# Media keys and values of all rows inside the integer attention, media statistics row by row, two buffers of routed rows

## The chip, the cores and the metric

The kernel runs on one core of a Trainium2 chip. The metric is the device time of one execution in microseconds (us), the median of three runs: 3255.36 us, from 3247.82 to 3256.58. The engines are named as in the profile: PE (TensorE, matmuls), PEld (its weight loads), DVE (VectorE), ACT (ScalarE), POOL (GpSimd) and SP (SyncE, which here only issues DMAs).

## What is computed

A decoder layer stack on `x` of 8 batch rows x 512 tokens x 256 channels, all in fp32. Every step adds to `x` what it computes from a layer norm of `x`:

```python
x = x + self_attention(LN(x))
x = x + cross_attention(LN(x), ctx_1024, adj, mask)
x = x + local_transformer(LN(x))              # depth 2, with feed-forward
x = x + integer_attention(LN(x))              # 16 heads, over the batch axis
x = x + media_attention(LN(x), ctx_1024, key_mask)
x = x + mixture_of_experts(LN(x))             # top 1 of 8, capacity 512, FF 1024
```

The change lies in the fourth and the fifth step, and in the routing that opens the sixth. The two that matter, cut:

```python
# integer attention (T = 8 rows, B = 512 tokens, E = 256)
xq, xs = quant_act(query, 8)                  # scale by the maximum over all of it, round
q, k, v = quant_linear(xq, ...) ; each quantized by its own maximum
aw = quant_act(einsum('ntd,nsd->nts', q, k)) ; probs = quant_act(int_softmax(aw))
attn = quant_act(einsum('nts,nsd->ntd', probs, v)) ; out = quant_linear(attn, wo)

# media attention (8 heads of 64; its own layer norm on top of the outer one)
xn = (x - mu) * rsqrt(var + eps) * gamma + beta
q = xn @ Wq * scale ; k, v = split(media @ Wkv)       # media = ctx_1024
out = softmax(mask(q k^T)) v @ Wout
```

Keys and values of the media attention depend on `ctx_1024` and `Wkv` alone, and not on `x`: they can be computed at any time once those are loaded. Each maximum in the integer attention is one over the whole tensor, so each of its sub-stages ends before the next begins.

## The kernel before

One core works through the stages one after the other in `fast_stages` (L3201). Of interest are `stage_quantized_attention` (L2257), `stage_media_attention` (L2664), `routing` (L2867) and `stage_moe` (L3018). `x` stays on the chip as 32 tiles of 128 tokens, four to a batch row. Engines have their own in-order instruction streams; a program schedules the order within each stream at build time, and semaphores join them. Tiles come from pools with a set number of buffers: a new tile of a name waits until the one that used its buffer is done with.

**The integer attention** is split by its pools:

- qa1/qp1: `rows` (L2298) makes integer rows of the normalised `x` (POOL and DVE L2307, DVE L2311, ACT L2312), transposes them on PE (L2315) and copies them by ACT (L2319). `channels` (L2284) multiplies them by the integer weights in PSUM tiles `pj` (3 buffers); `largest` (L2324) takes their maxima on DVE (L2326). Then queries, keys and values.
- qa2/qp2: scores, with their maxima in `aw`, a tile of four quarters' room that is first written here.
- qa3/qp3: `integer_softmax`, and in the same pools `keys_values` (L2586), which has nothing to do with it: it makes the *media* keys and values of batch rows 1 to 5 (`AHEAD`). Five contexts are loaded by SP into `qa_big`, a tile not yet in use. Then come 40 groups of two program matmuls on PE (L2608), each one evacuated by an ACT copy (L2610) into `kv_o` and stored in `kv`, a tensor in DRAM (L2611). One program matmul in fp32 of this kind appears in the trace as two records.
- qa4/qp4, the weighing phase: a loop of nine steps. `spread` (L2475) spreads values by POOL and DVE copies (L2478); `turn` (L2483) scales scores (DVE L2485), makes four shifted versions (ACT L2488), transposes them on PE (L2496) into PSUM tiles `tr` (4 buffers) and copies them back by DVE (L2499); `weigh` (L2501), one step behind, multiplies by the values (PE L2509), copies by ACT (L2517) and takes a maximum on DVE (L2518).
- qa5/qp5: rounding, transposes, and for each batch row b the output projection, its scaling by DVE into `qa_o` (L2575) and the addition to `x` (L2577), on DVE for odd b and on POOL for even b.

**The media attention** first takes the statistics of all 32 tiles (`ln_stats`: DVE L141, L142, then the inverse root in small operations, L1458 to L1462) and from them those of its second layer norm (L2684 to L2688). `prepare(b)` is a list of pieces of work for row b: `load` (the DMAs and the normalisation into `ma_xn`, L155), for rows 0, 6 and 7 the keys (four groups, L2726) and values (four groups, L2734), then two transposes (`turn`, L2713, and DVE L2719) and four groups of queries (L2726). For rows 1 to 5 the load reads `kv` from DRAM instead (L2701).

The loop runs 16 steps for each row. A step has the scores of a pair of heads for 128 keys (PE L2758), their exponent (ACT L2763) and the running sum: for the first of four steps a copy on POOL (L2769), else an addition on DVE (L2771). Two steps later PE weighs the values (L2781). In each step but the first, one piece of `prepare` for the next row is done. All of row 0's pieces run ahead of the loop, and the output projection and its addition to `x` (L2838, L2843) follow behind.

**The routing** of a row follows its output projection in pieces that fall due at set steps of the loop: statistics, the normalised rows into `mo_rows` (DVE L155; a copy of `x` and a count by POOL, L2906 and L2907), transposes, router logits (L2925), the choice of an expert, the place in it, and four indirect DMAs issued by POOL (L2988) that send the rows from `mo_rows` to `slots` in DRAM. `mo_rows` has one buffer. `stage_moe` reads `slots` when all sends are done.

Of the kernel before, what the change touches and what calls it, by code (L numbers as in the profile page):

```python
# [26 lines left out]
F32 = mybir.dt.float32  # L27
# [10 lines left out]
P = 128  # L38
# [1237 lines left out]
class FastDecoder(Decoder):  # L1276
# [980 lines left out]
    def stage_quantized_attention(self, w):  # L2257
# [3 lines left out]
        with tc.tile_pool(reuse_waits="tile", name="qa", bufs=1) as pool:  # L2261
# [17 lines left out]
            with tc.tile_pool(reuse_waits="tile", name="qa1", bufs=2) as tmp, tc.tile_pool(  # L2279
                reuse_waits="tile", name="qp1", bufs=1, space=PSUM  # L2280
            ) as psum:
                part = self.alloc(tmp, [P, B, 6], F32, "qa_part", bufs=1)

# [168 lines left out]
            with tc.tile_pool(reuse_waits="tile", name="qa3", bufs=2) as tmp, tc.tile_pool(  # L2452
                reuse_waits="tile", name="qp3", bufs=4, space=PSUM
            ) as psum:
                ptop = self.integer_softmax(tmp, aw, qs, atop)
                room = self.alloc(pool, [P, 8, 2, S], F32, "qa_big")
                self.keys_values(tmp, psum, room)

                ps_, _ = self.scaled(pool, ptop, 1.0 / 128.0 / 127.0, "qa_ps")
                pr = one("qa_pr")  # L2460
                nc.vector.reciprocal(pr, ptop)
                nc.vector.tensor_scalar(pr, pr, 127.0, None, ALU.mult)
# [7 lines left out]
            with tc.tile_pool(reuse_waits="tile", name="qa4", bufs=2) as tmp, tc.tile_pool(  # L2470
# [50 lines left out]

                for n in range(9):
                    if n < 8:
                        spread(n)
                        turn(n)
                    if n:
                        weigh(n - 1)

# [14 lines left out]
            with tc.tile_pool(reuse_waits="tile", name="qa5", bufs=2) as tmp, tc.tile_pool(  # L2543
# [22 lines left out]
                for b in range(B):  # L2566
# [10 lines left out]
                    (nc.vector if b % 2 else nc.gpsimd).tensor_tensor(x, x, o, ALU.add)  # L2577
# [6 lines left out]
    AHEAD = range(1, 6)  # L2584

    def keys_values(self, pool, psum, room):  # L2586
# [3 lines left out]
        self.kv = self.alloc(self.dram, [B, 2, P, NST * S], F32, "kv")  # L2590
        for n, b in enumerate(self.AHEAD):
            ctxT = room[:, n]
            nc.sync.dma_start(
                ctxT, t["ctxT"].rearrange("(k p) n -> p k n", p=P)[:, :, b * S : (b + 1) * S]
            )
        for n, b in enumerate(self.AHEAD):
            ctxT = room[:, n]
            for j in range(2):
                for g in range(NST):
                    ps = self.alloc(psum, [P, S], F32, "kv")  # L2600
                    for k in range(2):
                        at = slice(g * P, (g + 1) * P)
                        w, x = wkv[:, k, j * S : (j + 1) * S], ctxT[:, k, :]
                        if j == 0:
                            w = w[:, at]
                        else:
                            w, x = x[:, at], w
                        nc.tensor.matmul(ps, w, x, start=(k == 0), stop=(k == 1))  # L2608
                    o = self.alloc(pool, [P, S], F32, "kv_o", bufs=3)
                    nc.scalar.copy(o, ps)  # L2610
                    nc.sync.dma_start(self.kv[b, j][:, g * S : (g + 1) * S], o)  # L2611
# [52 lines left out]
    def stage_media_attention(self, w, out):  # L2664
# [5 lines left out]
        with self.tc.tile_pool(reuse_waits="tile", name="ma", bufs=2) as pool, self.tc.tile_pool(  # L2670
# [8 lines left out]


            mean, rstd, var = self.ln_stats(pool, lambda i: [self.x[:, i, :]], NT, "ma_ln", with_var=True)
            var2 = self.alloc(pool, [P, NT], F32, "ma_var2", bufs=1)
            rstd2 = self.alloc(pool, [P, NT], F32, "ma_rstd2", bufs=1)
            nc.vector.tensor_tensor(var2, var, rstd, ALU.mult)  # L2684
            nc.vector.tensor_tensor(var2, var2, rstd, ALU.mult)
            nc.vector.tensor_scalar(var2, var2, EPS, None, ALU.add)
            self.rsqrt(pool, rstd2, var2, "ma_t2")
            nc.vector.tensor_tensor(rstd2, rstd2, rstd, ALU.mult)  # L2688
            stats = mean, rstd2
# [3 lines left out]
            def prepare(b):  # L2693
                d = held[b] = {}

                def load():
                    d["k"] = self.alloc(pool, [P, 4, S], F32, "ma_kT")
                    d["v"] = self.alloc(pool, [P, NST, S], F32, "ma_v")
                    if b in self.AHEAD:
                        for j, n in enumerate("kv"):  # L2700
                            nc.sync.dma_start(d[n].rearrange("p a n -> p (a n)"), self.kv[b, j])  # L2701
                    else:
                        d["ctxT"] = self.alloc(pool, [P, 2, S], F32, "ma_ctxT")
                        nc.sync.dma_start(
                            d["ctxT"], t["ctxT"].rearrange("(k p) n -> p k n", p=P)[:, :, b * S : (b + 1) * S]
                        )
                    d["xn"] = self.alloc(pool, [P, NST, C], F32, "ma_xn", bufs=1)
                    for i in range(NST):
                        self.normalize(d["xn"][:, i, :], self.x[:, b * NST + i, :], stats, b * NST + i)
# [21 lines left out]
                def values(i):  # L2731
                    ps = self.alloc(psum, [P, 512], F32, "pj", bufs=2)
                    for k in range(2):
                        nc.tensor.matmul(  # L2734
                            ps, d["ctxT"][:, k, i * P : (i + 1) * P], wkv[:, k, S:],
                            start=(k == 0), stop=(k == 1),
                        )
                    self.evac(d["v"][:, i, :], ps)

                yield load  # L2740
                if b not in self.AHEAD:
                    for g in range(4):
                        yield lambda g=g: project(d["k"], wkv, d["ctxT"], g)
                    for i in range(NST):
                        yield lambda i=i: values(i)
# [120 lines left out]

    def routing(self, pool, psum, later, out):  # L2867
# [18 lines left out]
        def route(b):  # L2886
# [15 lines left out]
            def norm():  # L2902
                rows = d["rows"] = self.alloc(pool, [P, NST, self.WIDE], F32, "mo_rows", bufs=1)
# [466 lines left out]
```

## Time and profile before

| what | us |
| --- | --- |
| runs | 3247.82, 3256.58, 3255.36 |
| the profiled execution | 3254.52 |
| its span | 3252.6 |
| the 40 key and value groups of rows 1 to 5 (first to last ACT copy) | 2331.7 to 2399.8 |
| the weighing phase, qa4 | 2403.9 to 2442.4 |
| the last addition to `x` in the integer attention ends | 2481.1 |
| first scores of the media loop | 2511.64 |
| its rows open (POOL L2769) | 2515.33, 2555.63, 2608.16, 2663.18, 2718.19, 2774.16, 2843.62, 2913.08 |
| row 7's sends are issued | 3000.16 to 3005.0 |

Times count from the start of the span. In the page of the whole execution the engines are busy as follows (time, share of the span, number of instructions):

```profile
PE 2954.8 (91%) x15008; PEld 1502.6 (46%) x15008; DVE 2126.2 (65%) x4594; ACT 1148.2 (35%) x1599; POOL 415.7 (13%) x384
```

PE's share is a mean over all stages, of which some keep it full and some do not. Matmuls are pipelined and their ends are modelled, so what one takes out of the stream is read from the distance of two starts rather than from its length. An entry of the timeline or of the groups names the line, the engine, the operation, and what is written from what.

### The profile page before, as it was taken

Reading aid. Unit: us, or ns where it says so; the run is one execution under the profiler, and the core shown is the slowest. Engines: PE = TensorE matmul, PEld = TensorE weight load, DVE = VectorE, ACT = ScalarE, POOL = GpSimd, SP = SyncE. Lnnn points to the kernel's source line nnn. Section 1 sums busy time; section 2 is a strip of 40 time slices with the busy share of each in tenths; the row PEclk is TensorE's granted clock in tenths of the full one; section 3 lists DMA queues with packets and bytes.
Section 4 is the critical chain, followed back from the end, with each engine's and each line's share of the span. In section 5 each row is a group of like instructions: output and inputs, shape, how many; then the busy total and the mean of one; then the engine's idle time right before and its main releaser. Section 6 shows DMA issues by size and latency. Waiting matters only on the chain. (4 is left out here: it accounts for less than half of the span.)

```text
span 3252.6 us, 39809 instructions
## 1 busy us (share of the span) xinstructions
PE 2954.8 (91%) x15008; PEld 1502.6 (46%) x15008; DVE 2126.2 (65%) x4594; ACT 1148.2 (35%) x1599; POOL 415.7 (13%) x384
## 2 busy tenths in 40 slices
PE   8998888878998999999999999997876999996998
PEld 5642232224554555555454555554443333333665
DVE  6458888877878854466887858648798465555110
ACT  2146566643344321124334321113362443332111
POOL 1111001010011010000110111102211222222111
PEclk9999999989999999999999999998888999998999
DMA  7011111101000010001000011000321122112431
GB/s 230 1 58 44 57 52 39 39 16 53 15 21 21 17 46 14 1 1 37 17 21 15 21 41 59 20 7 26 105 86 46 53 99 79 34 35 78 121 135 58
DMA packets 122176, 155.82 MB, mean 48 GB/s; under 512 B 46742, under 2 KB 74477, under 8 KB 120694
## 3 DMA queue, kind: packets, MB, share of 16 engines
q1 hardware_dynamic: 117878, 141.59, 14.0%
q0 software_dynamic: 4096, 11.59, 1.0%
q8 instruction: 120, 1.97, 0.2%
q14 instruction: 82, 0.67, 0.1%
HBM read 106.66 MB, written 41.21 MB: 45 GB/s over the span
## 5 line engine op out<-in xcount | busy, mean ns | idle before, releaser
L1810 PE MATMUL pj<-w,la_hT 128*128 128x512 f32 x720 | 347.7, 615 | 23.4 <-DVE la_v L1815 21.2
L1662 DVE TENSOR_TENSOR x_e<-x_e,x_share 128x1024 f32<-128x1024 f32 x256 | 306.8, 1243 | 25.5 <-ACT x_e L1661 24.8
L1661 ACT ACTIVATE x_e<-sc 128x1024 f32<-128x1024 f32 x256 | 249.7, 1025 | 148.7 <-PE sc L1650 146.2
L2763 ACT ACTIVATE ma_e<-sc,ma_bias 128x1024 f32<-128x1024 f32 x128 | 142.4, 1114 | 200.9 <-PE sc L2758 192.6
L2771 DVE TENSOR_TENSOR ma_esum<-ma_esum,ma_e 128x1024 f32<-128x1024 f32 x96 | 122.4, 1275 | 134.9 <-ACT ma_e L2763 129.1
L1810 PEld LDWEIGHTS pj<-w,la_hT 128*128 128x128 f32 x720 | 129.8, 191 | 167.5 <-issue 119.3
L3113 POOL TENSOR_TENSOR la_oT<-la_o,x_wide 128x512 f32<-128x512 f32 x64 | 97.5, 1535 | 795.5 <-DMA x_wide<-invs 591.9
L1931 ACT ACTIVATE la_e<-la_e 128x1024 f32<-128x1024 f32 (+1 forms) x128 | 121.5, 951 | 182.5 <-DVE la_e L1927 182.5
L2095 ACT ACTIVATE lf_gate<-pj,lf_b 128x512 f32<-128x512 f32 (+1 forms) x82 | 56.3, 687 | 359.4 <-PE pj L2074 359.4
L1677 PE MATMUL po<-x_e,x_v 128*32 128x512 f32 x1024 | 143.5, 634 | 33.4 <-DVE x_e L1662 31.4
L2074 PE MATMUL pj<-lf_hnT,w 128*128 128x512 f32 (+1 forms) x368 | 173.5, 598 | 0.0
L1927 DVE TENSOR_TENSOR la_e<-sc,la_mask 128x1024 f32<-128x1024 f32 (+1 forms) x128 | 138.4, 1082 | 44.7 <-PE sc L1920 44.6
L1650 PE MATMUL sc<-x_q,x_k 32*128 32x512 f32 x1024 | 159.5, 663 | 0.3 <-ACT x_e L1661 0.2
L2074 PE MATMUL sc<-lf_hnT,w 128*128 128x512 f32 x336 | 155.9, 592 | 0.0
L2142 PE MATMUL po<-w,lf_hid 128*128 128x256 f32 x640 | 153.9, 386 | 0.0
L2758 PE MATMUL sc<-ma_qT,ma_kT 64*128 64x512 f32 x512 | 144.2, 641 | 0.7 <-ACT ma_e L2763 0.7
L1986 PE MATMUL pj<-w,la_oT 128*128 128x256 f32 x512 | 124.3, 389 | 22.0 <-ACT la_qkT L1856 12.6
L2781 PE MATMUL po<-ma_e,ma_v 128*64 128x512 f32 x512 | 138.1, 618 | 0.0
L1920 PE MATMUL sc<-la_qkT 64*128 64x256 f32 (+1 forms) x1024 | 134.2, 380 | 1.2 <-DVE la_e L1927 1.2
L2142 PEld LDWEIGHTS po<-w,lf_hid 128*128 128x128 f32 x640 | 117.3, 190 | 34.6 <-issue 20.4
L1938 PE MATMUL po<-la_e,la_v 128*64 128x256 f32 (+1 forms) x1024 | 129.0, 373 | 3.8 <-ACT la_o L1960 3.8
L1817 ACT ACTIVATE la_sq<-pj 128x512 f32<-128x512 f32 x120 | 71.4, 595 | 156.2 <-PE pj L1810 156.1
(486 smaller groups left out, 5206.3 us busy)
## 6 DMA issues: line engine op xcount, KB each, us to landing
x_wide<-invs SPq DMA_DIRECT2D x184, 128.0 KB
w<-in_f_w_dram SPq DMA_DIRECT2D x16, 1024.0 KB
kv<-kv_o SPq DMA_DIRECT2D x40, 256.0 KB
slots<-x_empty SPq DMA_DIRECT2D x8, 1028.0 KB
x_mask<-in_x_maskT_dram SPq DMA_DIRECT2D x8, 1024.0 KB
ex_rows<-slots SPq DMA_DIRECT2D x7, 1028.0 KB
ma_kT<-kv SPq DMA_DIRECT2D x5, 1024.0 KB
ma_v<-kv SPq DMA_DIRECT2D x5, 1024.0 KB
```

The costliest lines, as they stand in the source:

```text
L1650: nc.tensor.matmul(pair[r // 2][:, r % 2, :], d["k"][rows, g, kt * P : (kt + 1) * P], d["q"][rows, e, g, :], start=True, stop=True,)
L1661: nc.scalar.activation(ex, d["e"][rest][p], AF.Exp)
L1662: nc.vector.tensor_tensor(ex, ex, d["share"][:, kt, :].unsqueeze(1).broadcast_to([P, 2, 512]), ALU.mult)
L1677: nc.tensor.matmul(d["po"][32 * r : 32 * r + 32, :], d["v"][:, kt, 8 * g + 2 * r + e, :], ex[r // 2][:, r % 2, :], start=(kt == 0), stop=( ...
L1810: nc.tensor.matmul(ps, d["hT"][:, k, i * P : (i + 1) * P], wqkv[:, k, j * S : (j + 1) * S], start=(k == 0), stop=(k == 1),)
L1920: nc.tensor.matmul(ps[:, r, jj * 256 : jj * 256 + to - j * P], d["qkT"][rows, 4 + c, j * P : (j + 1) * P], d["qkT"][rows, c, j * P : to], ...
L1927: nc.vector.tensor_tensor(ex[:, :, :n_cols], ps[:, :, :n_cols], mask[:, :n_cols].unsqueeze(1).broadcast_to([P, 2, n_cols]), ALU.add,)
L2074: nc.tensor.matmul(ps[:m, :], w1[:, k, at : at + m], held[b]["hnT"][:, k, :], start=(k == 0), stop=(k == 1))
L2142: nc.tensor.matmul(ps[:, :C], src[:, i * P : (i + 1) * P], w2[: src.shape[0], f, :], start=(f == 0), stop=last_f,)
L2758: nc.tensor.matmul(ps[:, r, :], d["k"][rows, c, kt * P : (kt + 1) * P], d["q"][rows, c, :], start=True, stop=True,)
L2763: nc.scalar.activation(ex, ps, AF.Exp, bias=bias[:, b * NST + kt : b * NST + kt + 1], scale=0.125)
L2781: nc.tensor.matmul(d["po"][64 * r : 64 * r + 64, :], d["v"][:, kt, 128 * c + 64 * r : 128 * c + 64 * r + 64], ex[:, r, :], start=(kt == 0) ...
```

## The change

1. `keys_values` becomes a generator that takes the rows to do, the room for their contexts, the PSUM tag and the buffers, and that yields after each group. It is called three times:
   - for row 0 at the start of qa1, with PSUM tiles `pj`, two groups in each. The context lies in one quarter of the unused `aw`, and the ACT copies write the other three quarters in turn. That is 32 records on PE, four ACT copies of 128x1024, one context load and four stores on SP.
   - for rows 1 to 5 where it was, at once, as before.
   - for rows 6 and 7 in the nine-step loop of qa4, two groups in each step until the 16 are done, with PSUM tiles of the transposes' tag `tr`, `kv_o` in three buffers, and one buffer for the context.
2. The media loop loads keys and values of all rows from `kv`; its own groups for rows 0, 6 and 7 are gone.
3. The additions to `x` of the integer attention run on POOL for b = 2, 4, 6 and on DVE for the others.
4. The media statistics are taken for one row at a time (`twice_normal`): for row 0 directly after its addition to `x`, for rows 1 to 7 in their `load`.
5. `mo_rows` has two buffers (the pool's own number).

The core of the diff:

```diff
@@ stage_quantized_attention, qa1
+                self.kv = self.alloc(self.dram, [B, 2, P, NST * S], F32, "kv")
+                free = aw.rearrange("p n r a s -> p (n r a s)").rearrange("p (i k n) -> p i k n", i=4, k=2)
+                outs = itertools.cycle([free[:, i] for i in range(1, 4)])
+                for _ in self.keys_values(tmp, psum, range(1), free, "pj", 3, outs):
+                    pass
@@ qa3
-                self.keys_values(tmp, psum, room)
+                for _ in self.keys_values(tmp, psum, range(1, 6), room, "kv", 4):
+                    pass
@@ qa4
+                ahead = self.keys_values(tmp, psum, range(6, B), None, "tr", 4)
                 for n in range(9):
                     if n < 8:
                         spread(n)
                         turn(n)
                     if n:
                         weigh(n - 1)
+                    for _ in range(2):
+                        next(ahead, None)
@@ qa5
-                    (nc.vector if b % 2 else nc.gpsimd).tensor_tensor(x, x, o, ALU.add)
+                    (nc.gpsimd if b in (2, 4, 6) else nc.vector).tensor_tensor(x, x, o, ALU.add)
+                    if b == 0:
+                        self.media_stats = {b: self.twice_normal(tmp, b, self.const)}
@@ keys_values
+        if room is not None:
+            ctxs = [context(room[:, i], b) for i, b in enumerate(rows)]
+        for i, b in enumerate(rows):
+            if room is None:
+                ctxT = context(self.alloc(pool, [P, 2, S], F32, "kv_ctx", bufs=1), b)
+            else:
+                ctxT = ctxs[i]
             for j in range(2):
-                for g in range(NST):
-                    ps = self.alloc(psum, [P, S], F32, "kv")
...
+                for g in range(0, NST, n):
+                    ps = self.alloc(psum, [P, n, S], F32, tag, bufs=bufs)
...
+                    yield
@@ stage_media_attention
-            mean, rstd, var = self.ln_stats(pool, lambda i: [self.x[:, i, :]], NT, "ma_ln", with_var=True)
...
-                    if b in self.AHEAD:
-                        for j, n in enumerate("kv"):
-                            nc.sync.dma_start(d[n].rearrange("p a n -> p (a n)"), self.kv[b, j])
...
+                    for j, n in enumerate("kv"):
+                        nc.sync.dma_start(d[n].rearrange("p a n -> p (a n)"), self.kv[b, j])
+                    stats = self.media_stats.pop(b, None) or self.twice_normal(pool, b)
...
-                if b not in self.AHEAD:
-                    for g in range(4):
-                        yield lambda g=g: project(d["k"], wkv, d["ctxT"], g)
-                    for i in range(NST):
-                        yield lambda i=i: values(i)
@@ twice_normal (new)
+        mean, rstd, var = self.ln_stats(
+            pool, lambda i: [self.x[:, b * NST + i, :]], NST, "ma_ln", with_var=True
+        )
...
+        nc.vector.tensor_tensor(var2, var, rstd, ALU.mult)
+        nc.vector.tensor_tensor(var2, var2, rstd, ALU.mult)
+        nc.vector.tensor_scalar(var2, var2, EPS, None, ALU.add)
+        self.rsqrt(pool, rstd2, var2, "ma_t2")
...
@@ routing, norm
-                rows = d["rows"] = self.alloc(pool, [P, NST, self.WIDE], F32, "mo_rows", bufs=1)
+                rows = d["rows"] = self.alloc(pool, [P, NST, self.WIDE], F32, "mo_rows")
```

## The prediction, made before the changed kernel ran

> **What bounds the kernel now.** I read the busy times by stage first, because the mean (PE 91%) hides two regimes. Columns: window, its length, then for PE, weight load, DVE, ACT and POOL the busy time with its count, granted clock, DMA share, GB/s.
>
> ```profile
> 2200.50:2213.50 13.00, 0.00 (x0) 0.00 (x0) 7.92 (x30) 1.10 (x2) 1.10 (x2) 0.63 0.48 161
> 2213.50:2221.00 7.50, 5.64 (x30) 3.19 (x30) 6.55 (x12) 4.16 (x5) 2.80 (x1) 0.50 0.01 2
> 2403.00:2442.50 39.50, 19.51 (x640) 16.25 (x640) 34.35 (x50) 30.56 (x40) 13.38 (x13) 0.71 0.02 3
> 2481.00:2501.00 20.00, 14.07 (x26) 5.76 (x25) 19.25 (x98) 1.76 (x3) 0.37 (x2) 0.84 0.23 88
> 2516.00:2774.00 258.00, 257.38 (x1038) 92.05 (x1034) 148.49 (x294) 108.49 (x120) 63.00 (x57) 1.00 0.22 73
> 2774.00:2913.00 139.00, 139.00 (x523) 53.10 (x523) 72.67 (x152) 49.18 (x59) 30.35 (x28) 1.00 0.12 39
> ```
>
> The media loop (last two rows) has no idle PE time: a matmul removed there is time removed. At the start of the integer attention PE is idle for 13 us, in its weighing phase (2403 to 2442.5) it works half the time while DVE works 34.35 of 39.5, and in the prologue of media (2481 to 2501) DVE is the full engine. So the change moves PE work from a place where PE sets the end to places where something else does.
>
> Next, the timeline of POOL, whose copies open every head pair; these open rows 3 to 7:
>
> ```profile
> 2663.18 1.04 POOL L2769 COPY ma_esum<-ma_e 128x1024 f32<-128x1024 f32 x1 [8.40 <-ACT ma_e L2763]
> 2718.19 1.04 POOL L2769 COPY ma_esum<-ma_e 128x1024 f32<-128x1024 f32 x1 [8.40 <-ACT ma_e L2763]
> 2774.16 1.04 POOL L2769 COPY ma_esum<-ma_e 128x1024 f32<-128x1024 f32 x1 [8.21 <-ACT ma_e L2763]
> 2843.62 1.04 POOL L2769 COPY ma_esum<-ma_e 128x1024 f32<-128x1024 f32 x1 [15.46 <-ACT ma_e L2763]
> 2913.08 1.04 POOL L2769 COPY ma_esum<-ma_e 128x1024 f32<-128x1024 f32 x1 [15.76 <-ACT ma_e L2763]
> ```
>
> Row 3 takes 55.01 (2718.19 - 2663.18); rows 5 and 6, which prepare rows 6 and 7 with their own keys and values, take 69.46 and 69.46.
>
> Then the chain of waits at the end of the loop:
>
> ```profile
> 2797.20 1.91 PE pj L2734 x4
> 2931.83 4.07 DMA slots<-mo_rows,mo_to
> 2981.59 5.68 DMA slots<-mo_rows,mo_to
> ```
>
> The same places in the timelines (start, duration, what, in brackets the idle time before it and who ended it):
>
> ```profile
> 2936.06 0.15 POOL L2907 IOTA mo_rows<- 128x4 f32 x1 [2.81 <-DMA slots<-mo_rows,mo_to]
> 2987.40 2.18 DVE L155 TENSOR_SCALAR mo_rows<-x,mo_ln_mean,mo_ln_rstd 128x256 f32<-128x256 f32 x4 [9.82 <-DMA slots<-mo_rows,mo_to]
> 2500.92 1.38 DVE L155 TENSOR_SCALAR ma_xn<-x,ma_ln_mean,ma_rstd 128x256 f32<-128x256 f32 x4
> ```
>
> Twice the chain runs through the sends of routed rows, because the next row's `mo_rows` needs their buffer; and row 0's normalisation starts at 2500.92, 20 us after the last x add ended (2481.1).
>
> **Media loop, rows 6 and 7.** Their 16 groups leave a full PE. Measured by rows: 2 x (69.46 - 55.01) = **-28.9**. By the chain, 16 pieces like the first above, 16 x 1.91 = -30.6; I keep -26 (a tenth of it turning up as other waits) as the other end. The 2 x 2 loads of 1 MB replace two of 512 KB; rows 1 to 5 have such loads already and show no wait for them.
>
> **Two buffers of routed rows.** DVE's normalisation of row 7 (L155) stood 9.82 behind row 6's sends, till 2987.40. With a second buffer its inputs are ready at 2977.6: **-9.8** (-5 if the new sends queue behind row 6's on POOL, -10.5 at best). The stall at 2936.06, 2.81 behind row 5's sends, goes too: **-2.8** (0 to -4.1, the chain's piece). Late next: the router's matmuls, then row 7's own sends.
>
> **Prologue.** Before, DVE finishes the x adds at 2481.1, takes the statistics of all 32 tiles until 2493.6 and two inverse roots until 2500.9. After, DVE counts from its first qa_o at 2462.41: two qa_o 2.4; x rows 0 and 1 at 1.2 each, which is the same-shaped add L2771's price with POOL elsewhere, 2.4; four tiles' statistics at 0.39, 1.6; three pairs of (two qa_o 2.34 + an add beside POOL's, 2.35), 14.1; 27 small dependent operations at 0.20 (the pace of the 128x4 chain in the routing), 5.4. Sum 25.9, so xn at 2488.3, 12.6 earlier. PE then does no keys and values (they filled 2479.4 to 2503 and were hidden behind DVE), so it arrives cold: at 2494.4 half clock lasted 3.2 us after an idle gap, half of that lost, 1.6. Together **-11** (-6 if half clock holds through all 16 query records, +6.8, -12.6, say -13, without any).
>
> **Start of the integer attention, row 0's keys and values.** The context load (512 KB) stands on SP behind the first of the two 1 MB weights that wait for PE until 2200.5; the three share about 370 GB/s, so I let it land at 2206.8. 32 matmul records at 0.427 (the step at full clock) are 13.7; cold, the first 16 such records of the five-row pass took 9.94 instead of 6.8, +3.1: done 2223.6. The transposes of integer rows now stand behind them on PE: 16 of them 1.07, two ACT copies at 0.96, 1.9, six matmuls at 0.40, 2.4, gives the first DVE maximum at 2229.0 against 2225.41: **+3.5**. DVE sets the pace from there, so the delay passes on whole. Lower end 0 (landing 3.5 earlier, ahead of most of the weights' bytes), upper +8 (landing with the last of them at 2207.7, +0.9, and the second 16 records as slow as the first, +3.1: 7.5). The four ACT copies of 1.0 and four stores are covered: ACT works 4.16 of 7.50 there and SP issues nothing; uncovered they would be +4.
>
> The Trainium skill bears on that cold start: "TensorE: Matmul & The Clock Gate", in "Part 1: The HAM clock gate", says the gate releases after about 3.4 us of sustained work, and closes again after an idle window as long. It speaks against putting matmuls behind a 13 us gap, but would charge only half of 3.4, 1.7, where the row above shows 3.1; by it the sum would be 1.4 lower.
>
> **Weighing phase, rows 6 and 7's keys and values.** Built PE order: per step 16 transposes, two groups, 64 weighing matmuls. The 40 groups of the existing pass ran from 2331.7 to 2399.8, 1.746 each, clock 0.98. Per step: 2 x 1.746 + 1.07 (transposes at 2413.05) + 0.84 (weighing from 2415.93, two of 0.42) = 5.40, against 4.8 now (2403.9 to 2442.4 over 8). Eight steps from 2407.4: 43.2. Cold start, from the 3.1 above, 2.5 after the 7.72 us gap. Row 7's context has one buffer, so its load waits for row 6's last group; such a load took 3.7 (2475.69 to 2479.41), of which transposes and weighing cover 1.9: +2. Then the last copy and maximum, 1.0 + 1.4. End 2407.4 + 43.2 + 2.5 + 2 + 2.4 = 2457.5 against 2442.4: **+15**. Lower bound: if PE hides all, ACT still gets 16 x 0.585 = 9.4 on its 30.56 of 39.5, and with its old gaps filled ends no less than **+6** late. Upper: the groups share the four `tr` banks with the transposes, whose release waits for ACT behind four 0.80 us spreads; 16 more copies in series with the old step give 9.4, the same again in bank waits, and the load's whole 3.7, **+24** (22.5 rounded up). Evidence for the upper half:
>
> ```profile
> L2488 ACT ACTIVATE qa_wide<-qa_aw,qw_at_off,qw_at 128x512 bf16<-128x512 f32 x32 | 23.3, 803 | 4.1 <-DVE qa_aw L2485 4.1
> L2496 PE MATMUL tr<-qw_ident,qa_wide 128*128 128x128 bf16 x128 | 12.4, 274 | 8.4 <-ACT qa_wide L2488 8.4
> L2509 PE MATMUL po<-qa_h,qa_pT 128*32 128x64 bf16 x512 | 7.7, 212 | 12.4 <-DVE qa_pT L2499 12.4
> ```
>
> PE waits for ACT and DVE already, so everything is chained; yet PE's own gaps are 20 us, against 28 of new work, which supports the middle.
>
> **Statistics of rows 1 to 7** move into the loop on DVE. Some 13 us of small work falls between row 0's first running sums in the built order; DVE has 258 - 148 = 110 idle over the first loop window, and four `ma_e` buffers stand between DVE and ACT. **+1.5** (0 to +6: the part of 13 beyond about 7 us of buffers).
>
> **Sum**, on the profiled execution's 3254.5 (span 3252.6 plus 1.9 around it; 0.8 below the median): -28.9 - 9.8 - 2.8 - 11 + 3.5 + 15 + 1.5 = -32.5, so **3222**. All low ends together: -30.6 - 10.5 - 4.1 - 13 + 0 + 6 + 0 = -52.2, 3202. All high ends together, +1, would need every step to fail at once; weighing 9 over its value, first stage and statistics 4.5 each and the loop 2.9 give 20.9, 3243.
>
> **Rivals.**
> - *The additions hide* (start 0, weighing +6, statistics 0): -52.5 + 6 = -46.5, **3208**. For: PE has 13 and 20 idle us where they go. Against: ACT and DVE there are 77% and 87% busy, so not all fits. 0.13.
> - *The weighing phase runs in series* (+24) and the early sums are late (+6): -52.5 + 3.5 + 24 + 6 = -19, **3235.5**. For: the waits of the three groups just shown. Against: DVE and PE work in turn, leaving each gaps. 0.15.
> - *Slower: half clock in both new places.* For: 0.50 in the second window, 0.71 in the weighing phase. Start: 32 x 0.854 + 1.9 + 1.9 + 6 x 0.49 after 2206.8 gives 2240.9, +15.5. Weighing: 8 x 0.854 + 1.89 + 1.22 = 9.94 a step, 79.5 from 2407.4, +47. With 1.5 and -52.5: +11.5, **3266**. It turns slower once the additions pass 52.5. Against: the same matmuls in the five-row pass ran at full clock within 6 us of its start. 0.06.
> - *It doesn't do what it says*: rows 6 and 7 keep 69 us by another limit, -23.6 + 20 = -3.6, **3251**. Against: row 3 does the same other work in 55.01. 0.04.
>
> **How the numbers follow.** The forecast has 0.62. The range 3203 to 3243 holds it nearly whole, and the first two rivals; what is left out is the last two and tails of some 0.1. This kernel's measurement tells about 0.3%, 9.8 us, from no change: faster is below 3245.6. Faster 0.89 (forecast and two rivals, less a tail), same 0.05 (the fourth rival and that tail), slower 0.06.
>
> **What would show it.** Openings of all media rows 55 us apart; no wait of L155 for sends before row 7's; xn 26 us after the first qa_o (38.5 now); the first L2326 some 3.5 later; the weighing phase 53.5 us long. I would be wrong if the weighing phase passes 62 us, if a media row still takes over 60, or if granted clock there stays near 0.5.

## The result and the profile after

The changed kernel takes 3223.32 us (median of four runs, 3214.86 to 3225.10) against 3255.97 for the kernel before (four runs, 3247.82 to 3257.82): a ratio of 0.9899, 95% interval 0.9875 to 0.9924. The forecast was 3222, with a range of 3203 to 3243. The profiled execution has a span of 3222.1, 30.5 below that of before.

First the windows that answer to those of before (window, its length, busy time and count of PE, weight load, DVE, ACT, POOL, then granted clock, DMA share, GB/s):

```profile
2202.60:2208.80 6.20, 0.01 (x1) 0.00 (x0) 5.05 (x21) 0.00 (x0) 0.72 (x1) 0.71 0.79 286
2208.80:2225.00 16.20, 16.16 (x46) 7.48 (x47) 11.78 (x25) 5.63 (x6) 4.38 (x3) 0.90 0.39 150
2405.50:2458.00 52.50, 45.12 (x704) 25.78 (x704) 36.10 (x47) 38.86 (x56) 12.89 (x12) 0.90 0.28 97
2490.00:2519.00 29.00, 18.55 (x56) 9.30 (x55) 26.48 (x118) 3.69 (x5) 6.20 (x6) 0.71 0.11 36
2519.00:2780.00 261.00, 259.40 (x1049) 93.42 (x1049) 171.83 (x464) 109.29 (x120) 64.01 (x59) 1.00 0.22 76
2780.00:2890.00 110.00, 110.00 (x454) 41.72 (x453) 67.55 (x144) 44.20 (x50) 29.27 (x28) 1.00 0.22 78
```

The window around the weighing phase (third row) has grown from 39.5 to 52.5, and PE is now busy for 45.12 of it, where it was 19.51 of 39.5; e8 below tests whether PE has become its bound. The last row is the stretch of the media loop that took 139 us before and takes 110 now, with PE full in both. DVE's work in the loop's first part rose from 148 to 172 for the row statistics, and PE is still full.

Then POOL's copies that open rows 3 to 7:

```profile
2669.83 1.04 POOL L2764 COPY ma_esum<-ma_e 128x1024 f32<-128x1024 f32 x1 [8.28 <-ACT ma_e L2758]
2724.85 1.04 POOL L2764 COPY ma_esum<-ma_e 128x1024 f32<-128x1024 f32 x1 [8.29 <-ACT ma_e L2758]
2779.87 1.04 POOL L2764 COPY ma_esum<-ma_e 128x1024 f32<-128x1024 f32 x1 [8.29 <-ACT ma_e L2758]
2835.22 1.04 POOL L2764 COPY ma_esum<-ma_e 128x1024 f32<-128x1024 f32 x1 [8.30 <-ACT ma_e L2758]
2890.51 1.04 POOL L2764 COPY ma_esum<-ma_e 128x1024 f32<-128x1024 f32 x1 [8.30 <-ACT ma_e L2758]
```

Rows 2 to 6 now take 55.0 to 55.4 each, and the two that took 69.46 take 55.35 and 55.29. Rows 0 and 1 are shorter, as before (43.33 and 52.56, before 40.30 and 52.53), so the sign "openings of all media rows 55 us apart" holds for rows 2 to 6 only.

What each stretch gained or lost, from mark to mark within the two profiled executions (us):

| from | to | before | after | difference | forecast |
| --- | --- | --- | --- | --- | --- |
| start of the span | weights issued at the end of the local transformer | 2200.51 | 2202.64 | +2.1 | 0 |
| weights issued | first maximum, qa1 | 24.90 | 26.11 | +1.2 | +3.5 |
| first maximum | first transposes of the weighing phase | 182.01 | 180.62 | -1.4 | 0 |
| first transposes | maximum over the output (`qa_mpart`) | 35.02 | 50.49 | +15.5 | +15 |
| that maximum | first `qa_o` | 19.97 | 19.46 | -0.5 | 0 |
| first `qa_o` | first `ma_xn` | 38.51 | 24.14 | -14.4 | -12.6 |
| first `ma_xn` | row 0 opens | 14.41 | 15.48 | +1.1 | +1.6 |
| row 0 opens | row 5 opens | 258.83 | 260.93 | +2.1 | +1.5 |
| row 5 opens | row 7 opens | 138.92 | 110.64 | -28.3 | -28.9 |
| row 7 opens | row 6's first send | 64.62 | 67.24 | +2.6 | -2.8 |
| row 6's first send | row 7's first send | 22.46 | 12.03 | -10.4 | -9.8 |
| row 7's first send | end of the span | 252.44 | 252.32 | -0.1 | 0 |

The first row is not the change's doing: up to there the instruction order on each engine is the same in both, and in a second profile of the changed kernel (e9 below) the mark lies at 2200.03. In the profiles of this study it lies anywhere from 2196.9 to 2208.6. So single terms are compared from mark to mark within an execution; there, two profiles of the changed kernel agree within 0.3 us in every stretch but this first one.

In the experiments' kernels the stretches that hold the large terms repeat where the edit does not touch them: the weighing phase with both rows' groups takes 50.2 to 50.8 (48.9 in e6), `qa_o` to `ma_xn` 24.1 to 24.2, rows 5 and 6 together 110.0 to 110.7, row 7's opening to row 6's first send 67.2 to 67.3, and the two sends are 12.0 apart. Others do not repeat: the start with row 0's groups takes 26.1 to 27.9, and the third row of the table, whose instructions are the same in all of them but e6, 179.2 to 183.6. The +1.2 and the -1.4 of the table are therefore not settled by one profile of each kernel.

### The profile page after: what moved, and what is told of

Read it like the earlier page. It is cut to its first block, busy times and chain, and to the rows that moved or that the text cites. A ratio compares the mean times of both kernels' runs of the same rounds, so it can differ in the third digit from the quotient of the medians.

```text
span 3222.1 us, 40035 instructions
## 1 busy us (share of the span) xinstructions
PE 2949.9 (92%) x15008; PEld 1504.2 (47%) x15008; DVE 2143.2 (67%) x4766; ACT 1154.4 (36%) x1607; POOL 410.2 (13%) x383
## 3 DMA queue, kind: packets, MB, share of 16 engines
q8 instruction: 120, 1.97, 0.3%
## 5 line engine op out<-in xcount | busy, mean ns | idle before, releaser
L1987 PE MATMUL pj<-w,la_oT 128*128 128x256 f32 x512 | 124.3, 389 | 21.7 <-ACT la_qkT L1857 12.6
```

## The experiments

Each kernel is the changed one with one edit, unless said otherwise. Ratios are to the kernel before, run on the same chip in the same session. e12 and e13 had a profile and one time only.

| run | time | ratio (95% interval) | the stretch it was made for |
| --- | --- | --- | --- |
| e9, changed kernel again | 3221.42 | 0.9903 (0.9883 to 0.9923) | as above within 0.3 us |
| e2, one buffer of routed rows | 3238.99 | 0.9940 (0.9920 to 0.9960) | row 7 opens to row 7's first send: 87.8 (79.3) |
| e3, rows 6 and 7 made in the loop | 3236.05 | 0.9935 (0.9914 to 0.9955) | weighing 35.5 (50.5); rows 5 and 6 138.9 (110.6) |
| e4, statistics at once | 3231.37 | 0.9913 (0.9892 to 0.9934) | first `qa_o` to first `ma_xn`: 37.1 (24.1) |
| e6, row 0 with rows 1 to 5 | 3231.87 | 0.9923 (0.9900 to 0.9945) | weights issued to `qa_mpart` 265.2 (257.2) |
| e7, two products on DVE | 3217.72 | 0.9887 (0.9870 to 0.9905) | row 7 opens to row 6's first send: 63.7 (67.2) |
| e8, row 7 in the projection loop | 3208.30 | 0.9858 (0.9836 to 0.9880) | weighing 35.1 (50.5) |
| e10, e7 and e8 together | 3211.62 | 0.9867 (0.9842 to 0.9891) | both |
| e11, e10 with four groups moved | 3215.86 | 0.9875 (0.9851 to 0.9898) | `qa_mpart` to first `qa_o`: 26.0 (19.5) |
| e12, additions split as before | 3219.76 | | first `qa_o` to first `ma_xn`: 24.2 (24.1) |
| e13, all additions on DVE | 3223.42 | | the same: 23.5 (24.1) |

In brackets, the changed kernel's own value.

**e3: does the loop's gain come from PE, and the weighing phase's loss from the groups?**

```diff
-                ahead = self.keys_values(tmp, psum, range(6, B), None, "tr", 4)
...
-                    for _ in range(2):
-                        next(ahead, None)
...
+                if b >= 6:
+                    for g in range(4):
+                        yield lambda g=g: project(d["k"], wkv, d["ctxT"], g)
+                    for i in range(NST):
+                        yield lambda i=i: values(i)
```

> The changed kernel with the keys and values of rows 6 and 7 made in the media loop again, and none in the weighing phase. Theory (the loop is bound by PE, the weighing phase takes the 16 groups for 15.5): rows 5 and 6 of the loop take 69.5 again, + 28.3, the weighing phase 38.5, - 15.5; 3223 + 12.8 = 3236. Rival A (the loop became shorter for another reason, such as the loads from DRAM or the row statistics): rows 5 and 6 stay near 55 to 60, time 3208 to 3215. Rival B (the weighing phase grew for another reason than the groups): it stays above 50, time about 3250.

POOL's copies that open rows 6 and 7 in this run (row 5 opens at 2764.13):

```profile
2833.58 1.04 POOL L2781 COPY ma_esum<-ma_e 128x1024 f32<-128x1024 f32 x1 [15.49 <-ACT ma_e L2775]
2903.04 1.04 POOL L2781 COPY ma_esum<-ma_e 128x1024 f32<-128x1024 f32 x1 [15.65 <-ACT ma_e L2775]
```

69.45 and 69.46: the old row length to the hundredth, although the loads and the row statistics of the change are kept. The weighing phase falls to 35.45, 15.0 less. The net by marks is 28.3 - 15.0 = 13.3, and the ratio gives (0.9935 - 0.9903) x 3256 = 10, with an interval of some 6.5 on each of the two. From the first maximum to row 7's first send the run takes 16.3 more; the other 3.0 lie in stretches that the edit does not aim at, 2.5 of them ahead of the weighing phase, where the granted clock was 0.89 in place of 0.95. The theory holds, both rivals fall.

**e8: what bounds the weighing phase?** Only row 6's groups stay in it, one in each step; row 7's follow one after each row's projection.

```diff
-                ahead = self.keys_values(tmp, psum, range(6, B), None, "tr", 4)
+                ahead = self.keys_values(tmp, psum, range(6, 7), None, "tr", 4)
...
-                    for _ in range(2):
-                        next(ahead, None)
+                    next(ahead, None)
...
+                ahead = self.keys_values(tmp, psum, range(7, B), None, "tr", 4)
                 for b in range(B):
...
+                    next(ahead, None)
```

> The changed kernel with one group in each step of the weighing phase (row 6 alone), and row 7's eight groups in the projection loop behind it, one after each batch row's projection. Theory (PE sets the pace of the weighing phase: 2 groups 3.42, transposes and weighing 1.75 make 5.17 a step, and the second context is waited for 3.0; with one group it is 3.5, below the 4.8 that DVE and ACT took before): the phase falls from 50.5 to 39 to 41, the projection loop hides its eight groups in 24 us of DVE work, and PE is not cold at the media loop's first queries, 2 less: 3223 - 11 = 3212, from 3209 to 3215. Rival A (ACT's copies or the shared banks set the pace of the phase): it falls in proportion to the groups, - 7.5, and the context's wait, 3215 to 3217. Rival B (the groups delay the projections): 3220 or more.

First the steps as they run on PE in the changed kernel, with two groups each (start, duration, operation):

```profile
2417.35 3.70 PE L2627 MATMUL tr<-kv_ctx,w 128*128 128x512 f32 x8
2420.89 1.06 PE L2503 MATMUL tr<-qw_ident,qa_wide 128*128 128x128 bf16 x16
2421.87 0.69 PE L2516 MATMUL po<-qa_h,qa_pT 128*32 128x64 bf16 x64
2422.49 3.70 PE L2627 MATMUL tr<-w,kv_ctx 128*128 128x512 f32 x8
...
2436.35 5.37 PE L2627 MATMUL tr<-kv_ctx,w 128*128 128x512 f32 x8 [2.98 <-DMA kv_ctx<-in_ctxT_dram]
```

One step is 5.14 (2417.35 to 2422.49), back to back with no gap; row 7's context is waited for 2.98, and the groups behind that wait run slower, 5.37 in place of 3.70 (granted clock 0.68 from 2436.4 to 2441.8). The same in e8, one group a step:

```profile
2428.18 1.98 PE L2628 MATMUL tr<-w,kv_ctx 128*128 128x512 f32 x4
2430.46 1.27 PE L2503 MATMUL tr<-qw_ident,qa_wide 128*128 128x128 bf16 x16 [0.29 <-ACT kv_o L2633]
2431.66 0.69 PE L2516 MATMUL po<-qa_h,qa_pT 128*32 128x64 bf16 x64
2432.28 1.98 PE L2628 MATMUL tr<-w,kv_ctx 128*128 128x512 f32 x4
```

Steps of 4.1, with short waits for ACT (the three steps before them took 3.4 each, with none). The phase takes 35.1, as long as with no groups at all (35.0). The first eight groups are free, and the second eight bring all of the 15.4. Of these, 2.98 are the wait for row 7's context and 1.67 the slow groups behind it; some 10.8 are left for PE's own steps, less than eight groups at 1.71 (13.7), because the later steps with one group still had gaps. That fits a PE bound; a pace set by ACT's copies (rival A) would have left half the loss, and PE would show gaps between the groups. It is also better than the theory's own 39 to 41. The last part of the theory fails: the groups in the projection loop were not quite hidden (`qa_o` to `ma_xn` 26.8 against 24.1), and PE's first queries stayed slow (below). The stretch from the first maximum in qa1 to row 7's first send is 728.2 us long, 12.8 less than in the changed kernel.

**e2: what were the two buffers worth?**

```diff
-                rows = d["rows"] = self.alloc(pool, [P, NST, self.WIDE], F32, "mo_rows")
+                rows = d["rows"] = self.alloc(pool, [P, NST, self.WIDE], F32, "mo_rows", bufs=1)
```

> The changed kernel with one buffer of routed rows again, all else kept. In the changed kernel row 7's normalisation no longer waits for row 6's sends (gain 9.8), but at the first stall, where POOL's product no longer waits for row 5's sends, the tail lost 2.4 in place of gaining 2.8. Theory (the stall moved: POOL's three operations now run against DVE's running sum, which PE waits for): with one buffer both waits come back and the collision goes, so row 7's first send comes 7 to 8 us later, and the time is 3223 + 7.5 = 3231. Rival A (each stall is worth its length, and the 2.4 is something else of the change): + 12.6, 3236. Rival B (the sends never set the end): 3223.

From row 7's opening to its first send it takes 87.8, the changed kernel 79.3: +8.5, where the two waits that come back add up to 13.3 (L156 behind the sends 10.04, POOL 3.25). Row 6's first send comes 65.1 after row 7 opens, 2.2 *sooner* than with two buffers. So one of the two removed waits paid its full length, and the other had turned into something worse. The theory said 7 to 8 later. By the clock the whole time moved by more: the ratio is 0.0037 above that of e9, some 12 us, nearer to rival A's 12.6, but with an interval of 0.002 on each it does not tell 8.5 from 12.6. The marks do: under rival A row 6's first send could not come sooner. The other stretches from the weights' mark on differ by up to 1.8 and cancel (8.2 longer in all to row 7's first send). Rival B falls.

**e7: what is it that took the first wait's place?** DVE, POOL and PE in the changed kernel, where POOL is no longer held up behind row 5's sends:

```profile
2910.36 6.04 DVE L2766 TENSOR_TENSOR ma_esum<-ma_esum,ma_e 128x1024 f32<-128x1024 f32 x2
2910.69 1.29 POOL L3129 TENSOR_TENSOR ma_oT<-ma_o,x_wide 128x512 f32<-128x512 f32 x1
2911.90 1.06 POOL L2764 COPY ma_esum<-ma_e 128x1024 f32<-128x1024 f32 x1
2912.90 1.27 POOL L3129 TENSOR_TENSOR ma_oT<-ma_o,x_wide 128x512 f32<-128x512 f32 x1
2915.32 1.97 PE L2817 MATMUL sum<-ma_esum,ones 128*64 128x512 f32 x4 [2.17 <-DVE ma_esum L2766]
```

Two running sums that take 1.22 each elsewhere take 6.04. The first has 4.91 of it and ends at 2915.27, 1.1 after the last of POOL's three operations; the second, begun at 2915.19, takes its usual 1.21. PE waits 2.17 for the first. The edit moves the two products to DVE:

```diff
-        later.add(2, lambda: nc.gpsimd.tensor_tensor(out, o, wide, ALU.mult))
+        later.add(2, lambda: (eng or nc.gpsimd).tensor_tensor(out, o, wide, ALU.mult))
...
+                            nc.vector if b == B - 2 and c == 3 else None,
```

> The changed kernel with the two products of row 6's last head pairs (normally on POOL, directly after row 5's sends) on DVE; two buffers of routed rows stay. Theory (the freed POOL operations stretch DVE's running sum from 1.2 to over 4 us, and PE waits 2.2 for it): the sum takes about 1.2 again, PE does not wait, and row 6's first send comes 65 us after row 7 opens, as in the run with one buffer, in place of 67.2; time 3223 - 2 = 3221. Rival (PE waits there for the order of its own instructions or for ACT): 67.2 stays, and DVE's extra work of 1.4 makes it 3224.

DVE in e7, at the same place:

```profile
2913.78 1.22 DVE L2766 TENSOR_TENSOR ma_esum<-ma_esum,ma_e 128x1024 f32<-128x1024 f32 x1
2914.91 1.52 DVE L3132 TENSOR_TENSOR ma_oT<-ma_o,x_wide 128x512 f32<-128x512 f32 x1
2916.82 1.23 DVE L2766 TENSOR_TENSOR ma_esum<-ma_esum,ma_e 128x1024 f32<-128x1024 f32 x1 [0.39 <-ACT ma_e L2758]
```

The sums take 1.22 and 1.23, and row 6's first send comes 63.7 after row 7 opens, 3.6 sooner than in the changed kernel, and more than the expected 2. The whole time's ratio (0.9887 against 0.9903) points the same way, within its interval. The rival, another cause of PE's wait, falls. The mark is firm: it lies at 63.7 in e7, e10 and e11, which have this edit, and at 67.2 to 67.3 in all runs that have two buffers, the products on POOL and rows 6 and 7 prepared ahead.

**e4, e12 and e13: what made the prologue shorter?** e4 undoes the row-by-row statistics and the split of the additions; e12 undoes the split alone; e13 puts all additions on DVE.

```diff
-                    (nc.gpsimd if b in (2, 4, 6) else nc.vector).tensor_tensor(x, x, o, ALU.add)
+                    (nc.vector if b % 2 else nc.gpsimd).tensor_tensor(x, x, o, ALU.add)
...
+            mean, rstd, var = self.ln_stats(pool, lambda i: [self.x[:, i, :]], NT, "ma_ln", with_var=True)
```

> The changed kernel with the statistics of all 32 tiles taken at once ahead of the media loop and the additions to x split as before; keys and values stay where the change put them. Theory (DVE's statistics are what the prologue waited for): the media rows' first normalisation comes 38.5 us after the first qa_o again, in place of 24.1, + 14.4; the loop gets back the 3 us of its first row; 3223 + 11.5 = 3234.5. Rival A (the prologue became shorter because PE no longer makes row 0's keys and values there): time within 3 us of 3223. Rival B (statistics in the loop cost more than they save): 3215 or less.

> The changed kernel with the additions to x of the integer attention split as before (DVE for odd rows, POOL for even ones, row 0 too); the statistics stay row by row. Theory (the prologue gained from the statistics, not from the split): row 0's addition takes 2.35 on POOL in place of 1.21 on DVE and its statistics start 1 to 2 later, but DVE has one addition less; the first normalisation comes 24 to 26 us after the first qa_o. Rival (the split gave most of the gain): 30 us or more.

> The changed kernel with all eight additions to x on DVE. In the changed kernel each of POOL's three additions goes with one small DVE operation that takes 1.3 in place of 0.16. Theory (DVE stands still for about 1.15 while a POOL addition runs, so handing it to POOL saves DVE nothing): the first normalisation comes 24 to 25 us after the first qa_o, as now. Rival (POOL's additions are free for DVE, the long small operations are something else): 3 x 1.2 = 3.6 later, 27.7.

In e4 the first `ma_xn` comes 37.1 after the first `qa_o` (2488.44 and 2525.56): +13.0 of the expected 14.4. Row 0 then runs 2.4 faster and PE's queries 1.5, so that row 1 opens 9.0 later, against the 11.5 expected. The ratio (0.9913 against 0.9903, some 3 us) is too coarse to show these 9 and by itself would allow rival A. The marks do not: PE makes no keys and values there in e4 either, and yet the stretch is long again. Rivals A and B fall. In e12 it is 24.2 and in e13 23.5: the statistics gave the gain, and the split gave none. That three additions of 2.35 on POOL relieve DVE of nothing shows in the changed kernel's own timelines of POOL and DVE, where a small operation of 0.16 turns long beside each of them:

```profile
2486.67 2.36 POOL L2587 TENSOR_TENSOR x<-x,qa_o 128x1024 f32<-128x1024 f32 x1 [26.13 <-DVE ma_ln_mv L143]
2491.61 2.36 POOL L2587 TENSOR_TENSOR x<-x,qa_o 128x1024 f32<-128x1024 f32 x1 [2.58 <-DVE ma_ln_t L1461]
2496.41 2.34 POOL L2587 TENSOR_TENSOR x<-x,qa_o 128x1024 f32<-128x1024 f32 x1 [2.44 <-DVE ma_ln_t L1461]
2487.70 1.36 DVE L147 COPY ma_ln_mean<-ma_ln_mv 128x4 f32<-128x4 f32 x1
2492.66 1.33 DVE L1462 TENSOR_TENSOR ma_ln_t<-ma_ln_t,ma_ln_var 128x4 f32<-128x4 f32 x1
2497.46 1.31 DVE L1462 TENSOR_TENSOR ma_ln_t<-ma_ln_t,ma_ln_var 128x4 f32<-128x4 f32 x1
```

Each long operation ends within 0.03 us of POOL's addition (2489.06 and 2489.03, for the first). In the first half of each addition DVE did work: its scaling into `qa_o`, which reads PSUM, took its usual 1.2.

**e6: where is row 0 cheapest?**

```diff
-                for _ in self.keys_values(tmp, psum, range(1), free, "pj", 3, outs):
-                    pass
...
-                for _ in self.keys_values(tmp, psum, range(1, 6), room, "kv", 4):
+                for _ in self.keys_values(tmp, psum, range(6), room, "kv", 4):
```

> The changed kernel with row 0's keys and values made together with those of rows 1 to 5, six rows in one pass, and none at the start of the integer attention. Theory (the pass over five rows is bound by PE, 68 of 69 us busy; the start of the integer attention had 13 us of idle PE): the pass takes 8 x 1.71 = 13.7 more, the start 1 to 3 less; 3223 + 11 to 13 = 3235. Rival A (the integer softmax on DVE, 61 of 69 busy, sets that pass and hides the groups): 3220 to 3222. Rival B (the start cost the full 3.5 of the forecast and more down the line): 3223 + 13.7 - 3.5 to - 6 = 3231 to 3233.

The start gains 0.8 (weights issued to first maximum 25.3) and another 0.5 by the end of the maxima; the pass and the weighing phase behind it lose 9.3, and 2.0 of it come back between the maximum over the output and the first `qa_o`, so 6.0 remain there (6.2 at row 7's first send). Those 2.0 need not be the edit's: the granted clock in that stretch was 0.71 in place of 0.56, and e10, which does the same work there as e8, is 1.6 shorter than e8 at the same two clocks. The end of the integer softmax on DVE in this run:

```profile
2403.01 0.16 DVE L2680 TENSOR_REDUCE is_ptop<-is_ptops 128x1 f32<-128x4 f32 x1
```

and the last of its groups on PE:

```profile
2408.43 7.03 PE L2623 MATMUL kv<-w,qa_big 128*128 128x512 f32 x16
```

In the changed kernel the forty groups end on PE at 2401.65 and DVE's softmax at 2404.81, 3.2 later; with 48 groups PE ends 12.3 after DVE. So the eight more stick out, less those 3.2 and what the next phase overlaps, and the theory's 13.7 was too much. Rival A falls, and so does rival B: its time is near the measured one, but the start gave back 1.3 and not 3.5 to 6.

What row 0's groups cost at the start depends on the execution. Their first 16 records in the changed kernel and in e2:

```profile
2208.84 8.71 PE L2627 MATMUL pj<-qa_aw,w 128*128 128x512 f32 x16 [6.23 <-DMA qa_aw<-in_ctxT_dram]
2212.55 10.18 PE L2627 MATMUL pj<-qa_aw,w 128*128 128x512 f32 x16 [6.54 <-DMA qa_aw<-in_ctxT_dram]
```

The granted clock over them was 0.81 and 0.70. From the weights to the first maximum it then takes 26.1 and 27.9, against 24.9 before: a cost of 1.2 to 3.0, of which the changed kernel's profile shows the low end.

**e9, e10, e11: the reference, and a better version.**

> The changed kernel once more, beside the two others on the same chip, as their reference. All theories: 0.99 of the kernel before, and the same distances between marks of the media part within 0.5 us, whatever the executions differ by ahead of it.

> Both of the last two edits together: row 7's groups in the projection loop, and row 6's last two products on DVE. Theory (they act on two stages that follow one another, so they add): the weighing phase 35, row 6's first send 63.6 after row 7 opens, time 3222 - 10 to - 13 from the first and - 3.6 from the second, 3206 to 3209; ratio to the kernel before 0.984 to 0.986. Rival (one uses up what the other gains): 0.986 to 0.988.

> As the run before it, but only four of row 7's groups in the projection loop, one after every second row; the other four stand at the end of the weighing phase, where PE waits 8.7 us for the maximum over all of the output. Theory (in the projection loop PE needs 8 x (1.31 + 1.72) = 24.3, as much as DVE's 24.1, and so delayed the first normalisation by 2.6): the normalisation comes 24 us after the first qa_o again, the four groups fit behind the context's 3.7 in the gap but for 1 to 2 us; 1 to 2 us faster than the run before it. Rival (the four groups and their ACT copies come between the maximum and the rounding): the first qa_o comes 4 us or more later after the maximum than 19.4, and the time is 2 to 4 us longer.

By its ratio, 0.9867, e10 lies in the range of its rival (0.986 to 0.988), and its time is above the theory's 3206 to 3209. By marks it adds what e7 and e8 gave: from the first maximum in qa1 to row 7's first send it takes 723.2, against 728.2 in e8, 737.7 in e7, 741.0 in the changed kernel and 774.7 before. That is 17.9 less than in the changed kernel, where the two alone make 16.1; 1.6 of the difference is the stretch with the other clock named under e6. The interval (0.9842 to 0.9891) holds both readings. Its time, 3211.62, does not tell it from e8 (0.9836 to 0.9880, from another session); which of the two is faster by the clock stays open. Both beat the kernel before, and e8 beats the changed kernel of its session (0.9883 to 0.9923) by the clock too; e10's interval overlaps with that one, and its lead over the changed kernel rests on the marks. e11 fails by its rival: the four groups, waiting 3.07 for their context, take PE up to 2462.8 and ACT, between its roundings, up to 2463.6, in front of the rounding's transposes:

```profile
2454.22 8.70 PE L2633 MATMUL tr<-kv_ctx,w 128*128 128x512 f32 x16 [3.07 <-DMA kv_ctx<-in_ctxT_dram]
```

The first `qa_o` comes 6.6 later after the maximum.

## Why the prediction was right

The time (3223.3 against 3222) came from the forecast's own mechanisms, by the table of stretches, and in part by luck in how the small errors fell. Point by point:

- *Media loop, rows 6 and 7* (-28.9): measured -28.3, and e3 brings it back. Reading the row period from a steady-state row, rather than summing the removed matmuls, was enough because PE was full in all of it.
- *Weighing phase* (+15): measured +15.5. A step of 5.14 in place of 5.40, the context's wait of 2.98 in place of 2, and a slower stretch behind that wait which the sum did not have. e8 fits the bound on PE that the sum assumed, and shows that the cost is all in the second half of the groups, 4.7 of it the context's wait and the slow groups behind.
- *Prologue* (-11): measured -13.3. The chain from `qa_o` to `ma_xn` was shorter by 14.4 where 12.6 was said: the 14.1 for three pairs was priced at 2.35 for an addition beside POOL's, and DVE's took 1.21, but small operations took the delay instead. The cold queries cost 2.4 where 1.6 was said (first scores 13.1 after `ma_xn`, before 10.7), and part of that came back before the row opened.
- *Statistics in the loop* (+1.5): +2.1. Row 0 takes 3.0 longer, 2.0 of it PE waiting for row 1's normalisation at 2520.60; row 4 gives 0.9 back. e4 returns 2.4 in row 0.
- *Two buffers, second wait* (-9.8): -10.4, and e2 brings it back.
- *Start of the integer attention* (+3.5): +1.2 in this profile, up to +3.0 in others. The sum had the right chain, and the context landed at 2208.8, 6.2 after the weights were issued, as assumed. The first 16 records took 8.71 in place of the sum's 9.94, but 10.06 to 10.18 in e2, e4 and e8: here the cold start happened to be short.

One step was wrong in sign: "The stall at 2936.06, 2.81 behind row 5's sends, goes too: -2.8". The stall went, and the stretch became 2.6 longer. POOL's three operations, freed, ran against DVE's running sums, and PE waited for those; e2 and e7 show both sides of it. Without the collision, in e7, the stretch is 63.7 against 64.6 before: even then the 2.8 of POOL's wait were worth only about 1. The sentence named what would be late next on the path (the router's matmuls), but not what the earlier POOL work would run into. It missed by +5.4, and the execution's late start adds +2.1. Against that stand -2.3 at the start, -2.3 in the prologue, and -1.4 and -0.5 in two stretches that the forecast left at zero; the rest adds +1.0. The sum of the errors is +2.0 of a forecast change of -32.5. That is luck: the total is closer than the terms deserve.

The rival *the weighing phase runs in series* came nearest to deciding: PE did run in series there, but at the pace of the sum. *The additions hide* fell with the weighing phase's +15.5 in place of +6. *Half clock* did not come about: 0.90 was granted in both new places. *It doesn't do what it says* fell with rows 5 and 6 at 55.3.

## What to carry to other kernels

Work moved out of a full engine into the gaps of another stage is free up to the point where that engine is full there too, and then costs nearly its whole length: here eight groups cost nothing and sixteen 15.5 us, 4.7 of them for a second context that had to be waited for. So spread such work over several stages with gaps before filling one. And when a wait is removed, look at what the released engine will run against at its new time, because a wait off the main path can have been keeping two engines apart.

## What the runs showed of the hardware

- POOL work on large tiles can stop DVE rather than run beside it. A running sum of 1.22 on DVE took 4.91 beside three POOL operations, operations of 0.16 took 1.3 beside a POOL addition and ended with it, and e13 showed that three POOL additions of 2.35 saved DVE nothing (24.1 with them, 23.5 without). Not every operation is stopped: the scaling into `qa_o`, which reads PSUM, took its usual 1.2 beside the same additions. The Trainium skill, "SBUF — State Buffer", section "SBUF: two separate sides", has the rule: DVE and GpSimd share a pair of ports as an exclusive lock, held for the whole instruction. The small operations that ended with POOL's additions agree with it. The running sum shows one thing more: it is recorded as begun 0.33 us ahead of the first of POOL's three operations, while POOL was still issuing row 5's sends, and it waited for all three.
- PE's granted clock can fall to half without a long gap. In e8 the longest idle times of PE in the 11 us ahead of the first queries were 1.97, 1.44 and 1.19 us, and yet the 16 query records took 10.02, against 7.13 in the kernel before. Windows of e8 around them (the third number from the end is the granted clock):

```profile
2486.50:2488.00 1.50, 1.39 (x13) 1.26 (x13) 1.47 (x3) 0.00 (x0) 0.00 (x0) 0.95 0.22 86
2488.00:2492.00 4.00, 3.50 (x5) 0.99 (x4) 3.97 (x3) 0.42 (x1) 2.97 (x3) 0.59 0.00 0
2495.00:2500.00 5.00, 4.33 (x5) 1.85 (x6) 5.00 (x30) 0.51 (x1) 0.00 (x0) 0.50 0.99 365
```

  "TensorE: Matmul & The Clock Gate" of the Trainium skill, section "Part 1: The HAM clock gate", speaks of an idle window of about 3.4 us. No single gap here was that long; several short ones went with half clock all the same, and so did the one wait of 2.98 in the changed kernel's weighing phase (0.68 in the 5.4 us behind it).
- A stage's time moves between executions even where its instructions are the same, and the granted clock is part of it. From the first maximum to the first transposes of the weighing phase it took 179.2 us in e2 (clock 0.94), 180.6 in the changed kernel (0.95) and 183.6 in e11 (0.89); row 0 of the media loop took 43.3 at a clock of 1.00 in the changed kernel and 44.9 at 0.96 in e10. What lies ahead moved by up to 12 us (the weights' mark, 2196.9 to 2208.6) with the same instruction order. For terms of a few microseconds, marks within one execution tell more than whole times, and a term of 1 to 2 us needs more than one execution.
